# A three-layer graph network on one core: own rows on ScalarE's queue, rows home each six steps, the next team and W2 two steps later

## The chip, the core and the metric

The kernel runs on one NeuronCore of one Trainium2 chip. A core has five engines, each with its own instruction stream in fixed order: TensorE (PE, with the loading of its weights shown apart as PEld), VectorE (DVE), ScalarE (ACT), GpSimd (POOL) and SyncE (SP, which only issues DMAs here). They wait for each other through semaphores. Sixteen DMA engines move data between HBM and the on-chip memory (SBUF). Matrix products land in PSUM, which has eight banks.

The metric is the time of one execution in device microseconds, as the median of several runs.

## What is computed

A graph of 6250 nodes with 256 features and 100000 edges goes through three graph convolutions, and the result is added to the input and normalized:

```python
loops = jnp.arange(n)
src = concatenate([src, loops]); dst = concatenate([dst, loops])
deg = segment_sum(ones_like(dst), dst, n)
dinv = where(deg > 0, rsqrt(deg), 0)
norm_edge = dinv[src] * dinv[dst]
h = x
for W, b in ((W1, b1), (W2, b2), (W3, b3)):      # 256 -> 512 -> 512 -> 256
    h = relu(segment_sum((h @ W)[src] * norm_edge[:, None], dst, n) + b)
return layernorm(x + h)
```

Edges are sorted by `dst`. Each layer is a multiplication of a sparse matrix (edges and self loops) with the rows of all nodes, and one with a weight matrix; the kernel may take them in either order.

## The kernel before

**Tiling.** Nodes lie in 50 blocks of 125. The edges into one block are taken as 16 chunks of 128 edges. For a chunk POOL gathers 128 rows of the layer's table from HBM (L1306, an indirect DMA; in layer 2 a row has 512 numbers, 2 KB), and PE multiplies them with a one-hot matrix that sums them into the block's rows (L1334). To keep precision, ACT casts the gathered rows to a shorter float (L1366, the high half) and DVE subtracts that from the row (L1371, the low half); PE takes both, so a chunk is a pair of products.

**Dense blocks.** For some blocks the sparse matrix is counted out instead: a dense matrix of small integers, kept in HBM as bytes (`kept`). Then the block is a product with all 50 blocks of the table, which are streamed in order. In layer 2 the first 12 blocks are done so, as three *teams* of four (L916): for each source block k, four members get a pair of products (L1005), each into its team's bank. When a team is done, DVE scales its banks into SBUF (L940) and the next team may use them (`take`, L995). The other 38 blocks, 12 to 49, are gathered.

**A block in layer 2.** When a gathered block's sixteen chunks are summed, its *own rows* (the self loops) are added. They are loaded from the table into the one buffer `own_row` (L1321, when chunk j = 10 of the block's 16 is multiplied), scaled by ACT (L1345, with j = 15) and added by DVE (L1472). The next block's own rows can be loaded only then. After that come four transposes (L1426), an ACT copy (L1490), W2 in pairs of blocks (`hidden`, L1499; matmuls L1513), a relu on ACT (L1521), W3 (L1533), a scaling on DVE (L1548), and again a high and a low half (L1558, L1563). The result goes to the table of layer 3 (`tables[2]`) and, for use as dense operand in layer 3, to the SBUF tile `parts`.

**Returns.** While teams run, the upper part of `parts`, behind block 17, holds their buffers. Blocks past 17 that end in that time go to the table alone and come *home* (L1076) after the teams: 25 blocks in runs of up to four. Since the teams' slices and pieces lie in `parts` too, some instructions below carry that name while they move bytes of counts or halves of gathered rows.

**In advance.** Also after the teams, three dense blocks of layer 3 are begun early (`in_advance`, L1027): slices of their counts are loaded (L1036), cast on ACT (L1042, L1045) and multiplied (L1069) with the blocks of `parts` that are already there.

**Order.** All instructions are written by one loop. A *step* is one gathered chunk. Everything else is a generator that says after how many steps it wants to go on; `yield n` puts its next instructions n steps further along in the order of every engine. The constants are `SOON` = 2, `TO_PE` = 5, `LATE` = 6, `RETURN` = 6. In layer 2 a chunk's product stands 10 steps behind its gather; once the last team has six source blocks left, `returning` (L990) is set and the distance shrinks to 6. No cost model and no clock takes part: the order is fixed when the program is built, and at run time each engine waits for what it needs.

**DMA issue.** Most transfers of 125 rows go through `by_rows` (L81), which makes two of them, of 112 and 13 rows; the profile shows them under L85 and L87. Those of SP stand in SP's order, those of ACT in ACT's.

Of the kernel before, what the change touches and what calls it, by code (L numbers as in the profile page):

```python
# [26 lines left out]
Q = 125  # L27
# [4 lines left out]
SOON = 2  # L32
LATE = 6
TO_PE = 5

HOTS = 4
PIECE = 5
# [371 lines left out]
def sorted_path(ctx: ExitStack, tc: tile.TileContext, x, edges, starts, found, wts, biases, room, late, out):  # L409
# [65 lines left out]
    def take(name, most):  # L475
        while held.get(name, 0) >= most:
            yield 1
        held[name] = held.get(name, 0) + 1
# [437 lines left out]
    def teams(groups):  # L916

        nonlocal teams_done, returning
        units = [(g, k) for g in range(len(groups)) for k in range(NB)]

        def fetch_counts(g, c):
            for n, b in enumerate(groups[g]):
                by_rows(nc.sync, team_used[(g * CUTS + c) // 2 % 2][n].rearrange("p k v -> p (k v)"), kept[b][:, c * PIECE * Q:(c + 2) * PIECE * Q])

        def next_counts(g, c):
            if c + 2 < CUTS:
                fetch_counts(g, c + 2)
            elif g + 1 < len(groups):
                fetch_counts(g + 1, c + 2 - CUTS)

        def load(p):
            if 2 * p < len(units):
                k = units[2 * p][1]
                by_rows(nc.sync, streamed[p % RING], tables[1][k * Q:(k + 2) * Q, :].rearrange("(b p) c -> p b c", p=Q))

        def load_scales(g):
            nc.sync.dma_start(out=scales, in_=dinvs[g * TEAM:(g + 1) * TEAM, :].rearrange("b p -> (b p)").unsqueeze(0).to_broadcast([P, TEAM * Q]))

        def scaled(g, n):
            nc.vector.tensor_tensor(team_zt[:, n], team_banks[n][:, :TEAM * Q], scales, op=ALU.mult)  # L940
            free(f"team{n}")
            if n == TEAM - 1:
                if g + 1 < len(groups):
                    load_scales(g + 1)
                yield SOON
                team_ended[0](hidden(groups[g][:2], team_zt[:, :, :2 * Q], "tz"))
                for _ in range(4 * KF if g + 1 < len(groups) else 2 * KF):
                    yield 1
                team_ended[0](hidden(groups[g][2:], team_zt[:, :, 2 * Q:], "tz"))

        def piece(g, c, n):
            nc.scalar.copy(team_pieces[(g * CUTS + c) % 2][:, :, n * Q:(n + 1) * Q], team_used[(g * CUTS + c) // 2 % 2][n][:, c % 2 * PIECE:(c % 2 + 1) * PIECE, :])
            if c % 2 and n == TEAM - 1:
                next_counts(g, c - 1 + 2)

        def half(u, h):
            if u < len(units):
                to, row = both_parts[u % 3], streamed[u // 2 % RING][:, u % 2, :]
                if h == 0:
                    nc.scalar.copy(to[:, :HID], row)  # L960
                else:
                    nc.vector.tensor_sub(to[:, HID:], row, to[:, :HID].bitcast(F32))  # L962

        while products < FEW * NB - HOME // PIECE * PIECE:
            yield 1
        fetch_counts(0, 0)
        for p in range(RING):
            load(p)
        fetch_counts(0, 2)
        yield 6  # L970
        load_scales(0)
        while finished < FEW:
            yield 1
        for bank in team_banks:
            while not any(b is bank for b in common):
                yield 1
            del common[next(n for n, b in enumerate(common) if b is bank)]
        half(0, 0)
        for n in range(TEAM):
            piece(0, 0, n)  # L980
            if n % 2:
                yield 1
        half(0, 1)
        half(1, 0)
        yield 1
        half(1, 1)
        pairs_done = 0
        for u, (g, k) in enumerate(units):
            if u == len(units) - RETURN:
                returning = now  # L990
            if u % 2:
                load((u + 1) // 2 + RING - 1)
            for n in range(TEAM):
                if k == 0:
                    yield from take(f"team{n}", 1)  # L995
                if k == NB - 1 and n == 0:
                    while held.get("tz", 0):
                        yield 1
                    held["tz"] = TEAM // 2
                if 1 <= n < 3:  # L1000
                    half(u + 2, n - 1)
                if k % PIECE == 2 and u + PIECE < len(units):
                    piece(*divmod(g * CUTS + k // PIECE + 1, CUTS), n)
                for h in range(2):
                    nc.tensor.matmul(team_banks[n][:, :TEAM * Q], lhsT=both_parts[u % 3][:, h * HID + n * P:h * HID + (n + 1) * P],  # L1005
                                     rhs=team_pieces[(g * CUTS + k // PIECE) % 2][:, k % PIECE, :],
                                     start=(k == h == 0), stop=(k == NB - 1 and h == 1))
                if k == NB - 1:
                    team_ended[0](scaled(g, n))
                pairs_done += 1  # L1010
                if in_layer == 0 and pairs_done % 3 or in_layer == 1 and (pairs_done % PACE if now >= EAGER else pairs_done % 3 == 0):
                    yield 1
        teams_done = True
        assert not on_loan, (now, len(on_loan))
# [12 lines left out]
    def in_advance():  # L1027

        units = [(m, k) for k in ADVANCE for m in range(BEGUN)]
        banks = [mm_bank, mat_bank, tr_bank]  # L1030
        sliced = [(m, k) for m, k in units if m > 0]

        def load(u):
            if u < len(sliced):
                m, k = sliced[u]
                by_rows(nc.sync, early_slices[u % NS].rearrange("p k v -> p (k v)"), kept[many[m]][:, k * Q:(k + PIECE) * Q])  # L1036

        def convert(u):
            if u < len(units):
                m, k = units[u]  # L1040
                if m == 0:
                    nc.scalar.copy(early_pieces[u % 2], made[:, k:k + PIECE, :])  # L1042
                else:
                    n = sliced.index((m, k))
                    nc.scalar.copy(early_pieces[u % 2], early_slices[n % NS])  # L1045
                    load(n + NS)

        while returning is None:
            yield 1
        by_rows(nc.sync, made.rearrange("p k v -> p (k v)"), kept[many[0]])  # L1050
        for u in range(4):
            load(u)
        while not teams_done:
            yield 1
        for u in range(4, 9):
            load(u)
        while any(held.get(f"team{n}", 0) for n in range(TEAM)):
            yield 1
        for u in range(9, NS):
            load(u)  # L1060
        convert(0)
        yield 1
        sent = 0
        for u, (m, k0) in enumerate(units):
            while any(final.get(k, now + 1) > now for k in range(k0, k0 + PIECE)):
                yield 1
            convert(u + 1)
            for k in range(PIECE):
                nc.tensor.matmul(banks[m][:Q], lhsT=early_pieces[u % 2][:, k, :], rhs=parts[:, k0 + k],  # L1069
                                 start=(advanced[m] == 0), stop=False)  # L1070
                advanced[m] += 1
                sent += 1
                if sent % (2 if u < AT_HOME * BEGUN else AT_ONCE):
                    yield 1

    def home():  # L1076

        while not teams_done or held.get("leaving", 0):
            yield 1
        runs = []  # L1080
        for b in sorted(waiting):
            if runs and runs[-1][-1] == b - 1 and len(runs[-1]) < 4:
                runs[-1].append(b)
            else:
                runs.append([b])
        for run in runs:
            b, e = run[0], run[-1] + 1
            by_rows(nc.sync, parts[:, b:e].bitcast(F32), tables[2][b * Q:e * Q, :].rearrange("(b p) c -> p b c", p=Q))
            final.update((k, now + LANDING) for k in range(b, e))
            yield 4  # L1090

    there = []
    place_of = {}
# [63 lines left out]
    def layer(i, width, gathered, dense, after, rows, first=0, spacing=1.0, extras=(), carried=None):  # L1157
# [151 lines left out]
        def product(c):  # L1309
# [8 lines left out]
                    nc.tensor.matmul(acc[:Q], lhsT=ident_r[:Q, :Q], rhs=parts[:, b], start=True, stop=False)  # L1318
            if i == 1 and j == (3 if b == NB - 1 else KF - LATE):
                assert own_read == b - 1 or b == gathered[0]  # L1320
                by_rows(nc.sync, own_row, tables[1][b * Q:(b + 1) * Q, :])  # L1321
            several = [(j, split_rows.pop(c))]
            if j == KF - 1:
                several.append((KF, of_ten[b // GRP]))
# [174 lines left out]
    def hidden(two, zt, name, win=win_bank, ht2=ht2):  # L1499
# [1 line left out]
        wide = len(two) * Q  # L1501
        each = 4 // len(two)
        shares = win is win_bank
        yield TO_PE
        if shares:
            yield from take("ht2", 1)
        for f2 in range(0, KH, each):
# [348 lines left out]
```

## Time and profile before

| | us |
|---|---|
| median of 3 runs | 2067.19 |
| lowest and highest of them | 2065.59, 2067.45 |
| the profiled execution, its time | 2064.83 |
| its span, first to last instruction | 2063.2 |
| PE busy in it | 1926.2 |
| layer 2, first to last load of own rows | 727 to 1610 |

Times in the profile are in microseconds from the first instruction of the profiled execution. A row of a timeline has the start, the time taken, the engine, the line, the operation, what it writes and reads, and in brackets how long the engine stood idle before it and what ended that. An issue of a DMA is not work of its engine: it is marked with a q (SPq, ACTq), and the transfer ends later. A row of waits has who waited for whom, the total, the number of times and the longest. In a group's row stand the count and the busy time, or the least, the median and the greatest duration.

### The profile page before, as it was taken

The numbers are of one execution on the slowest core, as the hardware profiler recorded it, in microseconds if no ns is written. First come the engines' busy times: TensorE is split into PE (matmuls) and PEld (weight loads), VectorE is DVE, ScalarE is ACT, GpSimd is POOL, SyncE is SP. The second block draws the span as 40 slices with busy tenths as digits, with TensorE's granted clock in tenths as the row PEclk, the third lists the DMA queues.
The fourth block names the chain that finished last, engine by engine and source line by source line (L and its number), as shares of the span: only waits on it lengthen the run. The fifth ranks groups of instructions, "written<-read, shape, count | busy, mean of one in ns | idle before, by whom it ended". The sixth has DMA issues, their size and how long they took to land. (4 is left out here: it accounts for less than half of the span.)

```text
span 2063.2 us, 29141 instructions
## 1 busy us (share of the span) xinstructions
PE 1926.2 (93%) x8679; PEld 1521.4 (74%) x8679; DVE 1379.0 (67%) x2443; ACT 1279.3 (62%) x2255; POOL 1381.4 (67%) x1425
## 2 busy tenths in 40 slices
PE   4399999999999789999999989999889999999997
PEld 3277777777777557778888868888768778788886
DVE  6887888887882376677687676767746445444444
ACT  2566777787875466666676666666656555555553
POOL 2467777766777377777676676766757277777775
PEclk9999999999999899999999999999989999999998
DMA  7898999999999998999999998998997599999997
GB/s 171 246 300 220 264 266 259 272 264 254 276 274 248 250 280 255 267 262 265 263 263 265 263 261 249 267 254 253 266 278 221 151 288 292 289 294 299 290 284 203
DMA packets 266078, 535.53 MB, mean 260 GB/s; under 512 B 44363, under 2 KB 80328, under 8 KB 265910
## 3 DMA queue, kind: packets, MB, share of 16 engines
q0 software_dynamic: 155280, 355.58, 63.3%
q1 hardware_dynamic: 97194, 168.45, 30.3%
q10 hardware_dynamic: 13436, 9.55, 1.8%
q8 instruction: 70, 1.15, 0.2%
q14 instruction: 98, 0.80, 0.1%
HBM read 459.56 MB, written 73.87 MB: 259 GB/s over the span
## 5 line engine op out<-in xcount | busy, mean ns | idle before, releaser
L1306 POOL DMA_INDIRECT room<-tab,ssrc x442 | 456.4, 1033 | 199.8 <-issue 86.2
L1334 PE MATMUL sacc<-halves,shot 128*125 128x512 f32 x1524 | 519.9, 402 | 9.7 <-DMA halves<-tab,ssrc 4.7
L1255 ACT CAST piece<-room 125x625 fp32r<-125x625 uint8 x492 | 350.8, 721 | 187.4 <-PE win_ps L1407 53.0
L1306 POOL DMA_INDIRECT halves<-both,ssrc x384 | 360.5, 939 | 141.9 <-issue 42.4
L1306 POOL DMA_INDIRECT halves<-tab,ssrc x320 | 303.2, 947 | 98.8 <-issue 29.2
L1334 PEld LDWEIGHTS sacc<-halves,shot 128*125 128x125 f32 x1524 | 287.1, 189 | 84.3 <-DVE halves L1371 7.5
L811 DVE TENSOR_TENSOR back<-near_cols,slots 128x625 bf16<-128x625 f32 (+2 forms) x435 | 325.0, 803 | 31.5 <-PE sacc L878 12.4
L1371 DVE TENSOR_TENSOR halves<-room,halves 128x512 fp32r<-128x512 f32 x334 | 226.8, 692 | 121.2 <-ACT halves L1366 118.8
L1246 DVE TENSOR_TENSOR shot<-near_cols,sdlo 128x500 fp32r<-128x500 f32 x366 | 244.9, 670 | 93.2 <-PE sacc L1334 87.6
L1306 POOL DMA_INDIRECT back<-tab,ssrc x230 | 230.9, 1004 | 112.9 <-DVE halves L1371 35.1
L1366 ACT CAST halves<-room 128x512 fp32r<-128x512 f32 x334 | 202.0, 620 | 137.8 <-DMA room<-tab,ssrc 127.8
L1513 PE MATMUL win_ps<-back,w_sb 128*128 128x250 f32 x768 | 183.3, 382 | 9.1 <-ACT back L1490 8.6
L1513 PEld LDWEIGHTS win_ps<-back,w_sb 128*128 128x128 f32 x768 | 148.5, 194 | 33.5 <-ACT back L1490 11.0
L1407 PE MATMUL smm<-parts,piece 125*125 125x512 f32 x565 | 165.9, 409 | 2.1 <-DVE parts L1563 1.2
L1407 PE MATMUL win_ps<-parts,piece 125*125 125x512 f32 x550 | 158.2, 406 | 0.0
L1407 PE MATMUL str<-parts,piece 125*125 125x512 f32 x515 | 149.5, 408 | 0.9 <-ACT piece L1255 0.9
L878 PEld LDWEIGHTS <-back 128*125 128x125 bf16 x725 | 95.9, 138 | 73.3 <-issue 23.0
L1407 PE MATMUL sacc<-parts,piece 125*125 125x512 f32 x450 | 147.7, 432 | 0.9 <-ACT piece L1255 0.9
L840 ACT CAST room<-sacc 125x500 uint8<-125x500 f32 (+1 forms) x155 | 107.7, 713 | 55.3 <-PE sacc L878 40.8
L1371 DVE TENSOR_TENSOR halves<-back,halves 128x512 fp32r<-128x512 f32 x136 | 93.3, 693 | 61.1 <-ACT halves L1366 60.4
L1407 PE MATMUL mat_ps<-parts,piece 125*125 125x512 f32 x415 | 121.3, 408 | 0.4 <-ACT piece L1255 0.4
L962 DVE TENSOR_TENSOR parts<-parts 125x512 fp32r<-125x512 f32 x150 | 103.0, 687 | 25.5 <-ACT parts L960 24.8
(353 smaller groups left out, 3477.5 us busy)
## 6 DMA issues: line engine op xcount, KB each, us to landing
parts<-tab SPq DMA_DIRECT2D x75, 448.0 KB
kept<-room SPq DMA_DIRECT2D x29, 683.6 KB
room<-kept SPq DMA_DIRECT2D x27, 683.6 KB
both<-parts SPq DMA_DIRECT2D x10, 1120.0 KB
tab<-st SPq DMA_DIRECT2D x50, 224.0 KB
own_row<-tab SPq DMA_DIRECT2D x38, 224.0 KB
parts<-kept SPq DMA_DIRECT2D x60, 136.7 KB
room<-tab,ssrc POOLq DMA_INDIRECT x442, 6.2
```

The source lines that it names most:

```text
L811: nc.vector.tensor_tensor(out, near_cols[:, :shape[2]].unsqueeze(1).to_broadcast(shape), numbers.unsqueeze(2).to_broadcast(shape), op=ALU. ...
L840: nc.scalar.copy(place[:, :, u * G:(u + len(ms)) * G].rearrange("p k (t r) -> p t k r", r=G), counted_in[:Q, :len(ms) * 256].rearrange("p ...
L878: nc.tensor.matmul(bank[:Q, len(pair) * 256:][:, :G * NB], lhsT=hot_lo, rhs=hot_key, start=True, stop=True)
L962: nc.vector.tensor_sub(to[:, HID:], row, to[:, :HID].bitcast(F32))
L1246: nc.vector.tensor_tensor(hot[:, :n], near_cols[:, :Q].unsqueeze(1).to_broadcast([P, n, Q]), dlo.rearrange("p b j -> p (b j)")[:, at:at + ...
L1255: nc.scalar.copy(piece[:, :n], made_or_read[:, at:at + n, :])
L1306: nc.gpsimd.indirect_dma_start(out=row, out_offset=None, in_=table, in_offset=bass.IndirectOffsetOnAxis(ap=at, axis=0))
L1334: nc.tensor.matmul(acc[:Q, :size], lhsT=hot, rhs=row[:, c0:c0 + size], start=(i != 0 and k == c0 == 0), stop=(k == KF and c0 + size == row ...
L1366: nc.scalar.copy(halves[:, :width], landed[highs])
L1371: nc.vector.tensor_sub(halves[:, width:], landed.pop(lows), halves[:, :width].bitcast(F32))
L1407: nc.tensor.matmul(acc_d[:Q], lhsT=got[p][:, n, :], rhs=parts[:, k], start=begins and not (i == 2 and m < BEGUN), stop=ends)
L1513: nc.tensor.matmul(h_ps[:, f, :], lhsT=w2_sb[:, k, (f2 + f) * P:(f2 + f + 1) * P], rhs=zt[:, k, :], start=(k == 0), stop=(k == KH - 1))
```

## The change

Five edits in layer 2's order; no arithmetic changes.

```diff
             for n in range(TEAM):
                 if k == 0:
                     yield from take(f"team{n}", 1)
+                    if u and n == 0:
+                        yield SOON
...
         def load(u):
             if u < len(sliced):
                 m, k = sliced[u]
-                by_rows(nc.sync, early_slices[u % NS].rearrange("p k v -> p (k v)"), kept[many[m]][:, k * Q:(k + PIECE) * Q])
+                nc.sync.dma_start(out=early_slices[u % NS].rearrange("p k v -> p (k v)"), in_=kept[many[m]][:, k * Q:(k + PIECE) * Q])
...
             by_rows(nc.sync, parts[:, b:e].bitcast(F32), tables[2][b * Q:e * Q, :].rearrange("(b p) c -> p b c", p=Q))
             final.update((k, now + LANDING) for k in range(b, e))
-            yield 4
+            yield LATE
...
             if i == 1 and j == (3 if b == NB - 1 else KF - LATE):
                 assert own_read == b - 1 or b == gathered[0]
-                by_rows(nc.sync, own_row, tables[1][b * Q:(b + 1) * Q, :])
+                if returning is None:
+                    by_rows(nc.sync, own_row, tables[1][b * Q:(b + 1) * Q, :])
+                else:
+                    nc.scalar.dma_start(out=own_row, in_=tables[1][b * Q:(b + 1) * Q, :])
...
         each = 4 // len(two)
         shares = win is win_bank
-        yield TO_PE
+        yield TO_PE + SOON if shares and not teams_done else TO_PE
```

The second and the third team begin two steps later. The slices of counts come in one transfer of 125 rows each. A return follows the one before after six steps, not four. The own rows of the last seven blocks are asked for by ACT, in one transfer of 125 rows. And while teams run, W2 stands two steps further behind the transposes.

In the rows below, lines of the changed kernel are 2 to 5 higher than those of the kernel before: L1007 is L1005, L1044 and L1047 are L1042 and L1045, L1326 is the new load of own rows, L1339 is L1334, L1350 is L1345, L1371 is L1366, L1518 is L1513, L1563 is L1558.

SP's order where blocks come home, before. `parts<-tab_170` is a return of four blocks, `own_row<-tab_169` the load of own rows, `tab_170<-parts` the store of a pair of finished blocks:

```order
L87 DMA parts<-tab_170 112x4x512
L87 DMA parts<-tab_170 13x4x512
L87 DMA parts<-tab_170 112x4x512
L87 DMA parts<-tab_170 13x4x512
L87 DMA own_row<-tab_169 112x512
L87 DMA own_row<-tab_169 13x512
L87 DMA parts<-tab_170 112x4x512
L87 DMA parts<-tab_170 13x4x512
L85 DMA tab_170<-parts 112x2x512
L85 DMA tab_170<-parts 13x2x512
```

The own rows stand between the second and the third of these returns. The same place of SP's order in the changed kernel:

```order
L87 DMA parts<-tab_170 112x4x512
L87 DMA parts<-tab_170 13x4x512
L87 DMA parts<-tab_170 112x4x512
L87 DMA parts<-tab_170 13x4x512
L85 DMA tab_170<-parts 112x2x512
L85 DMA tab_170<-parts 13x2x512
L87 DMA parts<-tab_170 112x4x512
L87 DMA parts<-tab_170 13x4x512
```

The own rows are no longer between the returns. They stand in ACT's order now, here for the block whose own rows stood in the rows before. `halves` are casts of gathered rows:

```order
L1326 DMA own_row<-tab_169 125x512
L1047 CAST parts<-d 125x625
L1371 CAST halves_6034<-back 128x512
L1371 CAST halves_6035<-room 128x512
L1563 CAST parts<-st 125x2x256
L1371 CAST halves_6028<-room 128x512
L1044 CAST parts<-room 125x625
L1371 CAST halves_6029<-room 128x512
L1371 CAST halves_6030<-room 128x512
L1350 ACTIVATE own_row<-own_row,sdinv 125x512
L1047 CAST parts<-parts 125x625
```

Between the ask and the scaling stand five casts of gathered rows and three other instructions, and behind the scaling the cast of a slice for the early products. In the kernel before, no DMA stands in ACT's order here.

PE's order where the third team begins, before. `str` is the bank of the second team's last member, `sacc_893` that of the third team's first; `win_ps<-back,w_sb` is W2:

```order
L1005 MATMUL str<-parts 128x500 x2
L1334 MATMUL sacc_891<-halves_6028,shot_6023 125x512 x2
L1005 MATMUL sacc_893<-parts 128x500 x2
L1334 MATMUL sacc_891<-halves_6029,shot_6023 125x512 x2
L1513 MATMUL win_ps<-back,w_sb 128x250 x4
L1005 MATMUL mat_ps<-parts 128x500 x2
```

One pair of gathered products stands between the two teams, and W2 behind. In the changed kernel:

```order
L1007 MATMUL str<-parts 128x500 x2
L1339 MATMUL sacc_891<-halves_6030,shot_853 125x512 x2
L1518 MATMUL win_ps<-back,w_sb 128x250 x4
L1339 MATMUL sacc_891<-halves_6031,shot_853 125x512 x2
L1518 MATMUL win_ps<-back,w_sb 128x250 x4
L1339 MATMUL sacc_891<-halves_6032,shot_853 125x512 x2
L1007 MATMUL sacc_893<-parts 128x500 x2
```

Between the two teams stand three pairs of gathered products where one stood, and eight products of W2 that came behind the third team's first before.

## The prediction

> **What bounds the kernel now.** I read the page's busy line first, then busy time by stretch through the second layer, then what PE waited for there, then the timelines around the longest wait.
>
> ```profile
> PE 1926.2 (93%) x8679; PEld 1521.4 (74%) x8679; DVE 1379.0 (67%) x2443; ACT 1279.3 (62%) x2255; POOL 1381.4 (67%) x1425
> 700.00:930.00 230.00, 207.78 (x854) 161.12 (x852) 155.67 (x247) 146.65 (x265) 160.05 (x153) 0.96 0.90 259
> 930.00:1200.00 270.00, 267.41 (x1210) 222.98 (x1210) 198.10 (x314) 181.24 (x333) 189.81 (x187) 1.00 0.93 263
> 1210.00:1440.00 230.00, 230.00 (x1042) 193.31 (x1041) 166.09 (x264) 151.04 (x280) 159.59 (x156) 0.99 0.91 256
> 1500.00:1529.00 29.00, 28.99 (x131) 23.84 (x129) 16.49 (x26) 16.19 (x28) 18.30 (x19) 1.00 1.04 277
> 1529.00:1538.00 9.00, 0.05 (x1) 0.05 (x1) 0.67 (x1) 1.43 (x3) 0.00 (x0) 0.74 1.00 290
> 1538.00:1545.00 7.00, 7.00 (x22) 5.64 (x23) 5.04 (x9) 5.48 (x12) 4.37 (x5) 0.60 1.06 243
> 1545.00:1600.00 55.00, 55.00 (x251) 46.24 (x250) 32.93 (x53) 34.20 (x66) 39.45 (x39) 1.00 0.75 224
> ```
>
> The columns behind the stretch are busy time of PE, weight loads, DVE, ACT and POOL, then PE's granted clock, the DMA engines' busy share and GB/s. PE is busy nearly all the time from 930 us on, while DVE, ACT and POOL have a quarter or more to spare. So an idle microsecond of PE is a microsecond of the kernel, as long as what feeds PE can follow. The exceptions are the first stretch, where PE has other waits (22 us idle of 230), and the hole at 1529: nine microseconds in which PE does nothing while the DMA engines are full (share 1.00), then seven at a clock of 0.60. After it the DMA engines have room (0.75).
>
> ```profile
> PE str L1069 <- ACT parts L1045: 9.0, 1, 9.0
> PE win_ps L1513 <- ACT back L1490: 8.6, 6, 2.4
> PE sacc L1005 <- DVE back L940: 6.4, 2, 5.3
> PE sacc L1426 <- DVE szs L1472: 3.8, 3, 1.5
> PE smm L1069 <- ACT parts L1042: 3.7, 1, 3.7
> ...
> PE win_ps L1513 <- ACT back L1490: 5.6, 4, 2.4
> ```
>
> These are PE's waits in the second layer: total, times, longest (the last row: up to 930 us alone). Three of them are what the change speaks of: the hole (9.0), W2 waiting for the transposed rows (8.6 in six waits), and the next team waiting for DVE to empty its bank (6.4 in two).
>
> The hole's cause stands on SP's, ACT's and PE's timelines.
>
> ```profile
> parts<-tab SPq DMA_DIRECT2D x6, 896.0 KB
> parts<-tab SPq DMA_DIRECT2D x6, 104.0 KB
> ...
> 1503.71 8.79 SPq L87 DMA_DIRECT2D parts<-tab  x4
> 1514.50 1.57 SPq L87 DMA_DIRECT2D own_row<-tab  x2
> 1517.78 5.81 SPq L87 DMA_DIRECT2D parts<-tab  x2
> ...
> 1518.68 0.62 ACT L1366 CAST halves<-back 128x512 fp32r<-128x512 f32 x1 [1.14 <-DMA back<-tab,ssrc]
> ...
> 1524.41 0.62 ACT L1366 CAST halves<-room 128x512 fp32r<-128x512 f32 x1 [0.85 <-DMA room<-tab,ssrc]
> 1536.57 0.72 ACT L1345 ACTIVATE own_row<-own_row,sdinv 125x512 f32<-125x512 f32 x1 [11.54 <-DMA own_row<-tab]
> 1537.20 0.70 ACT L1045 CAST parts<-parts 125x625 fp32r<-125x625 uint8 x1
> ...
> 1528.35 0.64 PE L1334 MATMUL sacc<-halves,shot 128*125 128x512 f32 x2
> 1537.95 0.79 PE L1069 MATMUL str<-parts 125*125 125x512 f32 x1 [8.96 <-ACT parts L1045]
> ```
>
> The first two rows give the size of a return, about 1 MB in two transfers. SP asks for the own rows at 1514.50, behind two returns of 1 MB that were asked for from 1503.71 on. They have landed when ACT starts on them, 22 us later. ACT stops at its scaling, L1345, for 11.54 us, and everything ACT would have done next stops too: the casts of gathered rows, and the cast at L1045 for which PE waits. ACT's last cast ended at 1525.03 and PE ran dry at 1528.99, so PE carries 4.0 us of a stop of ACT: that cover is used below.
>
> That it is the queue and not the DMA engines alone shows in the gathers of the same stretch, which POOL issues on a queue of its own, about as large (128 rows of 2 KB):
>
> ```profile
> DMA to landing us min/median/max: 8.0/8.6/9.7
> ...
> DMA to landing us min/median/max: 3.4/4.1/7.5
> ```
>
> The first line is for the gathers asked for between 1500 and 1527, the second for those between 1540 and 1610. In the crowded stretch they land after 8.6 us, and the own rows after 22.
>
> The Trainium skill, "DMA: Bandwidth & Descriptors", section "Issuing engines are not separate DMA queues", speaks against this part of the change: all issuers share the same 16 engines, and asking from another saves only the time of issuing. By that rule the own rows would still land after some 22 us and T1 below would be nothing. The trace does not agree so far: 8.6 against 22 us in the same stretch, on two queues.
>
> **The change, part by part.** The sum is made against the profiled execution, 2064.83 us (span 2063.2); the median of the three runs lies 2.36 us above it.
>
> *T1, own rows on ACT's queue, and returns each six steps.* Seven of the 38 loads move, the ones after the last team nears its end. Gone is the hole, 8.96 us, and the slow stretch behind it: 7.00 us at 0.60 is 2.8 us lost. Together 11.8. What is late next? ACT now asks five steps ahead of its own use. In the rows above that is from 1518.68 (the fifth cast before) to 1525.03, 6.4 us. If the rows land as the gathers do, in 8.6 us, ACT waits 2.2 us, under the cover of 4.0; from 1540 on they land in 4.1 and nobody waits. No row shows how long one transfer of 125 rows takes; its bounds are the 3.4 us of the fastest gather and the 22 us of the old ask. I take the gathers' median, as the nearest in size, place and having its own queue. ACT also issues: seven times the row below, 2.5 us in all, on an engine that is idle for 21 of the 55 us after 1545.
>
> ```profile
> L85 ACTq DMA_DIRECT2D out<-st x100: 322/354/1030, 1661.1 to 2058.2; - x100
> ```
>
> The new ask stands in ACT's order, so it must also wait for DVE to have read the rows before (L1472). That read stands five to six steps earlier and so is done; behind the ask wait the casts, were it not.
>
> But 9 us of hole were not empty for the DMA engines: at 290 GB/s they moved 2.6 MB, mostly returns, which must now share the engines with gathers. With six steps between returns instead of four, some of that goes into the stretch at 0.75, where at 224 GB/s of the 290 seen there are 66 GB/s free, 3.6 MB in 55 us. It fits, though not all at the right time: I take two thirds of 11.8, **8 us**, with 0 and 11.8 as its ends.
>
> *T2, the next team two steps later.* It comes twice; the longer wait is the second row below. In two steps PE has two more pairs of products to do first:
>
> ```profile
> 1620.66 4.99 PE L1334 MATMUL sacc<-halves,shot 128*125 128x512 f32 x20
> 1208.05 1.18 PE L1005 MATMUL sacc<-parts 125*128 125x500 f32 x2 [5.35 <-DVE back L940]
> 1209.87 3.12 PE L1513 MATMUL win_ps<-back,w_sb 128*128 128x250 f32 x8
> ```
>
> Four at 0.25 us are 1.0 us of cover at each place: **2 us** of the 6.4. At 1208 the eight of W2 move ahead of the team too, but they need an ACT copy that is itself late there, so I count nothing for them. The ends are 0, if those products are late too, and 6.4.
>
> *T3, W2 two steps later.* Two steps hold two pairs of products and two pairs of the team's, 8 at about 0.25 us, 2.0 us of cover. The longest of the six waits is 2.4 us, so nearly all of 8.6 could go. Four of the six, 5.6 us, lie before 930, where PE has other waits close behind, so I take half, **4 us**; the ends are 0 and 8.6.
>
> *Nothing from the rest.* The 14 slices of counts are asked for in one transfer instead of two. SP saves 14 issues and half of the places in flight; their first use is far behind, some 47 us for the first four (rows below: asked from 1450, the first cast at 1497), and this hides a slower landing. The last team ends four steps later and the early products with it; PE has the same work, and the program still places all of it inside the second layer, whose last gathers' products fill PE to the end. The wait of 3.7 us for L1042 comes from a late gather in ACT's order ahead of it, during the first return, which stays: nothing.
>
> ```profile
> 1450.09 9.52 SPq L87 DMA_DIRECT2D d<-kept  x8
> 1486.68 0.83 SPq L87 DMA_DIRECT2D parts<-tab  x2
> 1494.90 0.62 ACT L1366 CAST halves<-room 128x512 fp32r<-128x512 f32 x1 [2.88 <-DMA room<-tab,ssrc]
> 1495.43 0.71 ACT L1042 CAST parts<-room 125x625 fp32r<-125x625 uint8 x1
> 1496.83 0.71 ACT L1045 CAST parts<-d 125x625 fp32r<-125x625 uint8 x1
> ```
>
> Sum: 8 + 2 + 4 = 14 us; 2064.8 − 14 = 2050.8, and on the median 2067.2 − 14 = **2053**.
>
> **The rivals.**
>
> *The wait only moves (no change).* If the DMA engines bound the whole end, the hole's 2.6 MB push the gathers back by as much. For it: shares of 1.00 to 1.06 from 1500 to 1545. Against it: 0.75 right after, and PE without a wait from 1500 to 1529 beside a share of 1.04. T1 gives nothing, and T2 and T3 vanish into the same queue: about 2065.
>
> *The change does not do what it says.* The own rows land as late from ACT's queue as from SP's: T1 is nothing, T2 and T3 stay: 2067.2 − 6 = 2061. The gathers' 8.6 us speak against it.
>
> *Slower: the ask blocks ACT.* One transfer of 125 rows may land later than two of 112 and 13, on top of the crowd, and ACT, in order, stops at L1345 once per block, seven times. PE loses what exceeds 6.4 + 4.0 = 10.4 us of landing. The change's other gains are 11.8 + 2 + 4 = 17.8, so it turns slower when PE loses over 2.5 us each time, with landings over **12.9 us**. At 15.4, midway from 8.6 to 22, PE loses 5 us seven times: 2067 + 35 − 18 = 2084. For it: 22 us have been seen for this very load. Against it: that was behind 2 MB on one queue, and four of the seven fall where gathers land in 4.1.
>
> The Trainium skill, same page, section "Why a DMA increments its semaphore by 16 and not by 1", gives a reason for this rival: a transfer is split over the largest number up to 16 that divides its slowest dimension, which is 5 engines for 125 rows and 16 for 112. No run here shows it. By that rule each of five engines carries 25 rows in place of about 8, an estimate of three times the data time, which in the crowded stretch would put the landing beyond the point that decides.
>
> **How the numbers follow.** The forecast, PE idle gone in part, 2040 to 2061: 0.70. The wait moves, 2063 to 2069: 0.13. The own rows as late as before, 2061: 0.07. ACT blocked, 2070 to 2090: 0.10. All three terms at their upper ends give 26.8 us, 2040. The range reaches from there, a microsecond lower, to 2067, and leaves out the slower case, the upper part of no change and a rest below. A measurement can tell about 0.2% from no change, 4.1 us. Faster: 0.70 + 0.07 = 0.77; within: 0.13; slower: 0.10.
>
> **What would show it.** Right: no PE wait over 3 us between 1500 and 1560 and no clock under 0.9 there; ACT's wait for own rows under 2.5 us each; `win_ps L1513 <- ACT back L1490` under 4 us in all; returns spread over some 50 us. Wrong: seven waits of ACT at its scaling, each over 4 us (the slower case); gathers that land in over 10 us until 1600 with PE waiting for casts (the wait moved); a PE hole before L1069 as long as now. A return landing after its first use would be a new wait, of PE for `parts<-tab`, that none of these cases holds.

## The result, and the profile after

| | us |
|---|---|
| kernel before, median of 12 runs | 2063.98 |
| changed kernel, median of 12 runs | 2072.83 |
| ratio of the runs, 95% interval | 1.0055 [1.0040, 1.0069] |
| the profiled execution after, its time and span | 2081.1, 2079.4 |

The change made the kernel slower, by about 9 us between the medians and by 0.55%, some 11 us, in the ratio of the runs. The forecast was 2053 us, and the time lies above its range. The profiled execution is 8 us slower than the median of its kernel, so it is read for where the waits are, and the sizes are taken from the ratios.

The busy line of the page and the stretches of layer 2's end, in the columns of the prediction:

```profile
PE 1936.2 (93%) x8679; PEld 1518.0 (73%) x8679; DVE 1379.7 (66%) x2443; ACT 1281.5 (62%) x2255; POOL 1384.4 (67%) x1425
1480.00:1501.00 21.00, 20.30 (x91) 16.05 (x89) 12.98 (x21) 10.32 (x19) 14.07 (x14) 1.00 0.94 252
1501.00:1512.00 11.00, 0.67 (x2) 0.35 (x3) 6.53 (x11) 4.22 (x8) 4.73 (x5) 0.67 0.70 227
1512.00:1519.00 7.00, 7.00 (x26) 5.73 (x27) 4.47 (x7) 4.14 (x8) 4.58 (x5) 0.79 0.60 147
1519.00:1553.00 34.00, 33.20 (x151) 27.08 (x150) 16.08 (x25) 17.79 (x32) 18.86 (x19) 1.00 1.04 270
1553.00:1580.00 27.00, 21.13 (x77) 15.69 (x76) 14.97 (x23) 14.00 (x26) 14.27 (x16) 0.87 0.79 226
```

The hole at 1529 is gone, PE works from 1519 to 1553 beside full DMA engines. But a hole of about the same length stands at 1501 and six more microseconds are missing after 1553. The new hole ends with the first of the early products, where the kernel before waited 3.7 us. And the second row has something that the old hole did not have: while PE waited, the DMA engines were at 0.70, where they had been at 1.00. So PE's wait did not come from 16 engines that were all busy.

PE's waits of 1480 to 1645 in the changed kernel, who waited for whom, the total, the times and the longest:

```profile
PE smm L1071 <- ACT parts L1044: 13.7, 2, 10.3
PE mat_ps L1071 <- ACT parts L1047: 2.3, 2, 1.6
```

ACT's wait for own rows there, and then ACT's timeline around the first three asks and scalings:

```profile
ACT own_row L1350 <- DMA own_row<-tab: 14.0, 3, 5.6
```

```profile
1497.23 0.26 ACTq L1326 DMA_DIRECT2D own_row<-tab  x1
1499.51 0.62 ACT L1371 CAST halves<-room 128x512 fp32r<-128x512 f32 x1 [1.68 <-DMA room<-tab,ssrc]
...
1504.17 0.62 ACT L1371 CAST halves<-room 128x512 fp32r<-128x512 f32 x1 [0.23 <-DMA room<-tab,ssrc]
1510.37 0.72 ACT L1350 ACTIVATE own_row<-own_row,sdinv 125x512 f32<-125x512 f32 x1 [5.58 <-DMA own_row<-tab]
1510.99 0.70 ACT L1044 CAST parts<-room 125x625 fp32r<-125x625 uint8 x1
...
1527.51 0.26 ACTq L1326 DMA_DIRECT2D own_row<-tab  x1
...
1540.89 0.72 ACT L1350 ACTIVATE own_row<-own_row,sdinv 125x512 f32<-125x512 f32 x1 [3.88 <-DMA own_row<-tab]
...
1557.69 0.26 ACTq L1326 DMA_DIRECT2D own_row<-tab  x1
1570.39 0.72 ACT L1350 ACTIVATE own_row<-own_row,sdinv 125x512 f32<-125x512 f32 x1 [4.54 <-DMA own_row<-tab]
```

And the row of PE's timeline that ends the hole:

```profile
1511.74 0.79 PE L1071 MATMUL smm<-parts 125*125 125x512 f32 x1 [10.33 <-ACT parts L1044]
```

Three of the seven own rows now stop ACT, for 14.0 us in all. From ask to scaling they took 13.1, 13.4 and 12.7 us, and each scaling began as its rows landed. The cast that PE waits for stands right behind the first of these scalings. ACT's stop is 5.6 us of the 10.3: PE had run dry at 1501.41, 3.4 us before ACT's last cast ended at 1504.79. The second stop cost PE almost nothing (33.20 of 34 us busy from 1519 on). PE's waits for casts of slices add up to 16.0 us (13.7 + 2.3) where they were 12.7 (9.0 + 3.7). The gathers, of 128 rows, landed in 8.2 and 9.1 us. The first row is for those asked for from 1485 to 1512, the second from 1512 to 1553:

```profile
DMA to landing us min/median/max: 6.4/8.2/8.8
DMA to landing us min/median/max: 3.9/9.1/10.6
```

### The profile page after: what moved, and what is told of

It is laid out like the page before. It is cut to its first block, busy times and chain, and to the rows that moved or that the text cites. A ratio compares the mean times of both kernels' runs of the same rounds, so it can differ in the third digit from the quotient of the medians.

```text
span 2079.4 us, 29088 instructions
## 1 busy us (share of the span) xinstructions
PE 1936.2 (93%) x8679; PEld 1518.0 (73%) x8679; DVE 1379.7 (66%) x2443; ACT 1281.5 (62%) x2255; POOL 1384.4 (67%) x1425
## 4 chain that ended last, share of the span: by engine, by line
PE 57%; DMA 17%; issue 10%; POOL 6%; ACT 4%; DVE 3%; SPq 0%; ACTq 0%; POOLq 0%; DVEq 0%
PE sacc L1339 10%; DMA room<-tab,ssrc 9%; PE smm L1412 6%; PE str L1412 6%; PE win_ps L1412 5%; PE sacc L1412 5%; DMA back<-tab,ssrc 4%; PE mat_ps L1412 4%; POOL room L1308 4%; PE win_ps L1518 3%; PE sacc L1457 2%; PE win_ps L1538 2%; POOL back L1308 1%; PE sacc L878 1%; DMA halves<-tab,ssrc 1%
## 5 line engine op out<-in xcount | busy, mean ns | idle before, releaser
L1339 PE MATMUL sacc<-halves,shot 128*125 128x512 f32 x1524 | 518.9, 401 | 11.9 <-DMA halves<-tab,ssrc 6.3
L1339 PEld LDWEIGHTS sacc<-halves,shot 128*125 128x125 f32 x1524 | 285.4, 187 | 89.2 <-DVE halves L1376 7.8
L1371 ACT CAST halves<-room 128x512 fp32r<-128x512 f32 x334 | 202.1, 620 | 148.3 <-DMA room<-tab,ssrc 133.7
L1518 PE MATMUL win_ps<-back,w_sb 128*128 128x250 f32 x768 | 186.0, 386 | 7.9 <-ACT back L1526 4.5
L1518 PEld LDWEIGHTS win_ps<-back,w_sb 128*128 128x128 f32 x768 | 149.7, 196 | 33.5 <-ACT back L1526 6.5
```

The lines of the kernel that those rows point to most:

```text
L1339: nc.tensor.matmul(acc[:Q, :size], lhsT=hot, rhs=row[:, c0:c0 + size], start=(i != 0 and k == c0 == 0), stop=(k == KF and c0 + size == row ...
L1371: nc.scalar.copy(halves[:, :width], landed[highs])
L1518: nc.tensor.matmul(h_ps[:, f, :], lhsT=w2_sb[:, k, (f2 + f) * P:(f2 + f + 1) * P], rhs=zt[:, k, :], start=(k == 0), stop=(k == KH - 1))
```

## The experiments

Four theories stood at the start. **Theory 1**: one transfer of 125 rows is slow by its shape and stops ACT. **Theory 2**: the slices in one transfer are slow in the same way, or make gathers late. **Theory 3**: the two shifts cost. **Theory 4**: the returns each six steps cost. The first kernels start from the change and undo one part, the later ones start from the kernel before and do one part. Runs of one group were on one chip; in the last three groups they were chips on which the kernel before takes 2259 to 2287 us, so only ratios within a group are compared there. In the traces from those chips PE also has waits for which the profile shows no cause (21.8 us before one line in own_128_shifts), so an effect need not have the same size on both kinds of chip.

### From the changed kernel: rows and slices

`own_two` (own rows on ACT's queue in two transfers):

```diff
-                    nc.scalar.dma_start(out=own_row, in_=tables[1][b * Q:(b + 1) * Q, :])
+                    by_rows(nc.scalar, own_row, tables[1][b * Q:(b + 1) * Q, :])
```

> After the change, but ScalarE asks for an own row in two transfers (112 rows and 13) in place of one of 125. Theory 1 (one transfer of 125 rows is itself slow: asked at 1497 to 1558 us it was there 13 us later, while gathers of 128 rows took 8 to 9): own rows land in 7 to 9 us, ACT's three waits at its scaling (14.0 us) shrink under 5 us, PE's hole of 10.3 us before L1071 shrinks, ratio to before 0.997 to 1.001. Theory 2 (the slices in one transfer make the gathers late from 1484 on, and the hole is theirs): the hole stays over 7 us, ratio 1.003 to 1.006. Theory 3 (the two-step shifts cost the time): own rows may land sooner, but the ratio stays at 1.004 or above and PE waits for ACT's relu before W2 stay at 8 us.

`slices_two` (the slices of counts in two transfers, as before):

```diff
-                nc.sync.dma_start(out=early_slices[u % NS].rearrange("p k v -> p (k v)"), in_=kept[many[m]][:, k * Q:(k + PIECE) * Q])
+                by_rows(nc.sync, early_slices[u % NS].rearrange("p k v -> p (k v)"), kept[many[m]][:, k * Q:(k + PIECE) * Q])
```

> After the change, but each slice of counts is asked for in two transfers (112 rows and 13), as before the change. Theory 2 (slices in one transfer make the gathers late): ACT's waits for gathers between 1485 and 1502 us (2.8, 2.4 and several of 1 us) fall to those of the kernel before, and the hole of 10.3 us shrinks under 4 us; ratio to before 0.997 to 1.002. Theory 1 (only the own row's single transfer): ACT still waits 4 to 6 us at its scaling, the hole keeps over 7 us, ratio 1.003 to 1.006.

`both_two` has both edits.

> After the change, with both own rows and slices in two transfers of 112 and 13 rows; what is left of the change is ScalarE's queue, the returns each six steps and the two shifts. Theories 1 and 2 together: no PE wait over 4 us between 1490 and 1560 us, ratio to before 0.992 to 0.998 (the 8 to 12 us of the hole). Theory 3 (the shifts cost) or a theory 4 (returns each six steps cost): ratio 1.002 or above although the waits for own rows are gone.

`own_128` (one transfer, three rows more; `own_row` is the first 125 rows of `own_full`):

```diff
-                    nc.scalar.dma_start(out=own_row, in_=tables[1][b * Q:(b + 1) * Q, :])
+                    wide = Q if b == NB - 1 else P
+                    nc.scalar.dma_start(out=own_full[:wide], in_=tables[1][b * Q:b * Q + wide, :])
```

> After the change, but ScalarE asks for 128 rows in one transfer (three more than are used; the last block 125), still one transfer. If it is the number of rows that makes it slow (125 rows dividing badly over the DMA engines; 128 evenly), own rows land in 7 to 9 us, as in two transfers, and ACT's waits at its scaling fall under 5 us in all. If it is one transfer as such, or ACT's queue, that is slow, they land after 12 to 14 us as in the changed kernel, and the ratio stays 1.004 to 1.007.

| kernel | median, us | ratio to before, 95% | ACT's waits for own rows in the profile, us |
|---|---|---|---|
| changed kernel | 2072.83 | 1.0055 [1.0040, 1.0069] | 14.0 |
| slices_two | 2071.72 | 1.0037 [1.0021, 1.0054] | 8.5 |
| own_two | 2066.91 | 1.0011 [0.9992, 1.0031] | 2.1 |
| both_two | 2066.60 | 1.0008 [0.9990, 1.0025] | 1.2 |
| own_128 | 2060.81 | 0.9981 [0.9962, 1.0001] | 1.7 |

Three rows more make the changed kernel 12 us faster (2072.83 − 2060.81, medians of two groups; the two ratios lie 0.74% apart). That is theory 1, and it is the number of rows, not one transfer as such. Slices in two change nothing beyond the intervals, alone or with the own rows: theory 2 is not the cause, though an effect of 0.1 or 0.2% would not show. Both_two was expected at 0.992 to 0.998 with no wait of PE over 4 us; it came out at 1.0008 with one of 7.3 us: with both mended the loss is gone, but the gain is still missing.

The traces put the difference at the end of layer 2. From the scaling of the ninth-last own row to that of the last, one execution each took 192.0 us in the kernel before, 199.7 in the changed kernel, 197.6 in slices_two, 191.5 in own_two, 190.0 in both_two and 189.9 in own_128.

Why three rows matter shows in the count of packets on ACT's DMA queue (q10), over the time in which one own row was moved. The view of the DMA queues has packets, MB and the share of 16 engines. In the changed kernel from 1532 to 1541 us:

```profile
q10 hardware_dynamic: 130, 0.26, 9.0%
```

In own_128 from 1528 to 1533:

```profile
q10 hardware_dynamic: 144, 0.26, 16.7%
```

In own_two from 1525.5 to 1530.5:

```profile
q10 hardware_dynamic: 154, 0.26, 19.7%
```

A row of 2 KB is one packet, so there are 5 packets beyond 125 rows, 16 beyond 128, and 29 = 16 + 13 beyond 112 + 13. The packets' times in the traces, for the same three loads:

```
                 rows  packets beyond  first to last packet, us  rows under way at once, at most
changed kernel    125        5                7.82                         5
own_128           128       16                4.12                        13
own_two           125       29                4.17                        12
```

So 125 rows in one transfer went over few engines, by the extra packets five with 25 rows each, and took about twice as long (8.04 and 7.74 us in the other two loads that stopped ACT). This load stood in the crowd of returns and gathers. Outside it up to 7 of the rows were under way at once and a load took 3.0 to 4.0 us, where own_128 had up to 18 and 1.3 to 2.4 us, and ACT was not stopped. The Trainium skill, "DMA: Bandwidth & Descriptors", section "Why a DMA increments its semaphore by 16 and not by 1", says that each engine in a transfer ends its part with a write to the semaphore, and that their number is the largest up to 16 that divides the slowest dimension: 5 for 125, 16 for 128 and 112, 13 for 13. The counts 5, 16 and 29 are those numbers: the trace agrees. The share of 0.70 fits too, but which engines were idle the trace does not tell.

PE's wait for L1044 from 1480 to 1645, in own_two:

```profile
PE smm L1071 <- ACT parts L1044: 8.7, 2, 6.6
```

and in own_128:

```profile
PE smm L1071 <- ACT parts L1044: 3.4, 2, 2.0
```

In own_two 6.6 us of hole are left at 1505 although ACT waited only 1.1 us for its own row. Most of its casts just before had waited 0.6 to 1.3 us each for a gather, behind the first return of 1 MB. That part of the hole is not the own rows'. This wait, of PE for the first early product, was 3.7, 2.9 and 4.9 us in the three kernels without the two shifts (before, own_128_no_shifts, own_128_alone). With the shifts it was 6.6 here, 7.5, 7.3 and 6.0 in slices_two, both_two and own_128_each_four, but 4.4 in shifts_alone and 2.0 in own_128. So the shifts are a suspect; what sets it was not tried.

### One part at a time

`shifts_alone` is the kernel before with the two shifts:

```diff
                     yield from take(f"team{n}", 1)
+                    if u and n == 0:
+                        yield SOON
...
-        yield TO_PE
+        yield TO_PE + SOON if shares and not teams_done else TO_PE
```

> The kernel before with the two shifts alone (next team and W2 two steps later); own rows, slices and returns as before. Prediction's terms T2 and T3: 6 us less, ratio 0.996 to 0.998. Rival (the wait only changes its name: W2 then waits for ScalarE's relu in place of its copy, some 8 us of the changed kernel's waits): ratio 0.999 to 1.002. Theory 3 (the shifts cost): 1.003 or above. The hole of 9 us at ScalarE's scaling of own rows stays in all three.

`own_128_no_shifts` is own_128 without these lines.

> As own_128, without the two shifts: own rows by 128 rows on ScalarE's queue, returns each six steps, slices in one transfer. If the shifts are worth their 6 us: ratio to before 1.000 to 1.003 (own_128 had 0.998). If they only change the name of a wait: 0.997 to 0.999, as own_128. If they cost: 0.994 to 0.996.

`own_128_each_four` is own_128 with `yield 4` between returns.

> As own_128, with returns each four steps as before the change. If the wider spacing carries the gain (the crowd of returns and gathers from 1500 us on): a PE hole of over 5 us comes back between 1500 and 1560 us, gathers land after 10 us or more there, ratio 1.000 to 1.004. If the own rows' queue alone removed the hole: PE's waits there stay under 4 us each, ratio 0.997 to 0.999.

`own_128_alone` is the kernel before with one edit:

```diff
-                by_rows(nc.sync, own_row, tables[1][b * Q:(b + 1) * Q, :])
+                if returning is None:
+                    by_rows(nc.sync, own_row, tables[1][b * Q:(b + 1) * Q, :])
+                else:
+                    wide = Q if b == NB - 1 else P
+                    nc.scalar.dma_start(out=own_full[:wide], in_=tables[1][b * Q:b * Q + wide, :])
```

> The kernel before with one edit: from the last team's end on ScalarE asks for own rows, 128 rows in one transfer. The prediction's T1 without the wider returns: the 11.5 us wait at ScalarE's scaling falls under 3 us, PE's hole of 9.0 us goes; ratio 0.995 to 0.998 (4 to 10 us of 2064). Rival (the DMA engines bound the end, the wait moves into gathers): own rows land in 6 to 8 us but PE waits as long for casts, ratio 0.999 to 1.001.

| kernel | median, us (before: 2062.98) | ratio, 95% |
|---|---|---|
| shifts_alone | 2067.02 | 1.0026 [1.0012, 1.0041] |
| own_128_no_shifts | 2058.72 | 0.9975 [0.9958, 0.9993] |
| own_128_each_four | 2060.28 | 1.0000 [0.9982, 1.0018] |
| own_128_alone | 2055.46 | 0.9974 [0.9960, 0.9987] |

`own_128_alone` beats both kernels. Its last nine scalings span 186.5 us, 5.5 less than before. PE's waits in it from 1480 to 1645:

```profile
PE smm L1069 <- ACT parts L1042: 4.9, 1, 4.9
PE sacc L1338 <- DMA halves<-tab,ssrc: 1.6, 1, 1.6
PE str L1069 <- ACT parts L1045: 1.4, 2, 1.1
```

and its gathers asked for between 1500 and 1527:

```profile
DMA to landing us min/median/max: 8.4/9.0/11.0
```

ACT waits 0.4 us for own rows in all. PE's wait of 9.0 has become 1.4, the other one stays (3.7 before, 4.9 now). The gathers land 0.4 us later than in the kernel before (9.0 against 8.6): the hole's bytes did not come back as late gathers. So the prediction's T1, with rows that land as gathers do, is real: 5.4 us by the ratio (0.26% of 2063, the interval from 2.7 to 8.3), where 8 were taken.

The shifts gain nothing: beside own rows of 128 there is no difference that could be told (0.9981 with, 0.9975 without, in different groups), and alone they cost 0.26% (its last nine scalings span 197.6 us, 192.0 before). The spacing of returns can't be told from nothing by these four. Own_128_each_four has a hole of over 5 us again, as its expectation said for the case that the spacing matters, but at 1496 and with no stop of ACT by own rows before it.

### Rows and queue

`own_125_alone` is own_128_alone with the change's own line (125 rows in one transfer on ACT's queue), `own_two_alone` has `by_rows(nc.scalar, ...)` there, `own_128_on_sync` has `nc.sync` in place of `nc.scalar`, and `own_128_home_six` adds `yield LATE` between returns.

> The kernel before with the own rows as the change asks for them and nothing else: from the last team's end on ScalarE asks for 125 rows in one transfer. Own_128_alone, three rows more, had 0.9974. Theory 1 (125 rows go over five DMA engines, land after 12 to 14 us and stop ScalarE): ScalarE waits 3 to 6 us at its scaling in three of seven blocks, ratio 1.002 to 1.006. Rival (ScalarE's queue is worth what it was with 128 rows, and the loss of the changed kernel needs the other edits): ratio 0.996 to 0.999.

> As own_128_alone, but the one transfer of 128 rows stays on SyncE's queue. If it is the queue that made the own rows late before (asked for behind 2 MB of returns): ScalarE still waits over 5 us at its scaling once or twice, ratio 0.999 to 1.002. If one transfer of 128 rows in place of two of 112 and 13 did it: waits under 2 us, ratio 0.996 to 0.998 as own_128_alone.

> As own_128_alone, but two transfers of 112 and 13 rows on ScalarE's queue. If the queue is what counts: own rows land in 7 to 8 us, ScalarE's waits stay under 2 us, ratio 0.996 to 0.999. If the single even transfer is needed (own_two had 1.0011 where own_128 had 0.9981): 0.999 to 1.002.

> Own_128_alone with returns each six steps. If the wider spacing helps (own_128 0.998 against own_128_each_four 1.000): ratio to before 0.994 to 0.996. If it is nothing: 0.9965 to 0.9985. If a return now lands after its first use (PE waited 4.4 us for it in own_128_no_shifts): such a wait of 3 us or more shows again, ratio 0.998 to 1.000.

Since the first two intervals hold no change, the first two came again on another chip, with 125 rows on SP's queue (`own_125_on_sync`, `nc.sync` in the change's line) and own_128_alone with the two shifts (`own_128_shifts`).

> Own_125_alone once more, beside the same load in three other forms on one chip. Theory 1 (125 rows on five DMA engines stop ScalarE): 1.002 to 1.006, ScalarE's waits at its scaling over 8 us in all. Rival (on ScalarE's queue 125 rows are as good as 128): 0.996 to 0.999, waits under 3 us.

> The kernel before with own rows of 125 in one transfer from the last team's end on, but on SyncE's queue. If rows and queue add: it lands after 22 us or later, as in the kernel before, and more often; ratio 1.002 to 1.008. If the queue alone decides (rows don't matter there, since all transfers wait behind the returns): 0.999 to 1.002, as before. If the number of transfers is what counts on SyncE: below 0.999, as own_128_on_sync.

> Own_128_on_sync on the chip of the three others. If the queue is what made the own rows late: they land 15 us or more after the ask and ScalarE waits over 5 us once; ratio 0.999 to 1.002. If one even transfer is enough on either queue: 0.996 to 0.999.

> Own_128_alone (0.9974) with the two shifts. If the shifts are worth the 6 us of the prediction's T2 and T3: 0.994 to 0.996. If they only rename waits: 0.996 to 0.999. If they cost, as shifts_alone's 1.0026 says: 0.999 to 1.001, with early products that end some 7 us later and the last two blocks of gathers 3 us longer.

| kernel | ratio, 95% (group with before at 2286.62) | ratio, 95% (group with before at 2258.65) |
|---|---|---|
| 125 rows in one, ACT's queue | 1.0016 [0.9996, 1.0036] | 1.0027 [1.0005, 1.0050] |
| 125 rows in one, SP's queue | | 1.0025 [1.0003, 1.0047] |
| 128 rows in one, SP's queue | 0.9987 [0.9964, 1.0011] | 1.0014 [0.9982, 1.0045] |
| 112 and 13 rows, ACT's queue | 0.9969 [0.9944, 0.9994] | |
| 128 rows, ACT's queue, returns each six | 0.9984 [0.9964, 1.0003] | |
| 128 rows, ACT's queue, shifts | | 1.0031 [1.0007, 1.0055] |

On ACT's queue the same rows make the kernel faster in two transfers and not in one of 125: 0.9969 against 1.0016 beside each other (0.9974 for 128, on another chip). On SP's queue 128 rows stay within their intervals of no change. Why, shows in asks and scalings. ACT's timeline in own_125_alone:

```profile
1669.30 0.26 ACTq L1324 DMA_DIRECT2D own_row<-tab  x1
1685.81 0.72 ACT L1348 ACTIVATE own_row<-own_row,sdinv 125x512 f32<-125x512 f32 x1 [8.11 <-DMA own_row<-tab]
```

SP's in own_128_on_sync, asks for two blocks:

```profile
1640.92 0.34 SPq L1325 DMA_DIRECT2D own_row<-tab  x1
1668.97 0.34 SPq L1325 DMA_DIRECT2D own_row<-tab  x1
```

and ACT's in the same run, their scalings:

```profile
1661.64 0.72 ACT L1349 ACTIVATE own_row<-own_row,sdinv 125x512 f32<-125x512 f32 x1 [1.35 <-DMA own_row<-tab]
1687.14 0.73 ACT L1349 ACTIVATE own_row<-own_row,sdinv 125x512 f32<-125x512 f32 x1 [2.91 <-DMA own_row<-tab]
```

125 rows landed 16.5 us after the ask (1669.30 to 1685.81), and 128 on SP's queue 20.7 and 18.2 us. So the change mended the queue and broke the shape: in the crowd either alone is enough to make the rows late. It is not so for each load. In own_125_alone this one of the seven stopped ACT, in its repetition again one, for 4.7 us, less than the 3 to 6 us in three blocks and the 8 us in all that were expected. The changed kernel and slices_two, with returns each six steps, had three stops each. On SP's queue 128 rows stopped ACT for 4.3 us in own_128_on_sync and 5.9 in its repetition. The Trainium skill, "DMA: Bandwidth & Descriptors", section "Issuing engines are not separate DMA queues", allows only the time of issuing as a gain from another queue. The traces speak against it here: even 128 rows took 18 to 21 us on SP's queue, behind returns asked for from 1631.85 and 1658.07 us on, and on ACT's, in own_128_home_six on the same chip, the rows for the same two blocks were scaled about 9 us after their asks (1669.25 to 1678.34, 1694.47 to 1703.52). In own_two_alone, also on that chip and with returns each four steps as in own_128_on_sync, it was 9.5 and 9.1 us.

The returns each six steps show no gain (0.9984 with 128 rows, beside 0.9969 with each four and 112 + 13 rows, in the same group). Theory 4 is not shown either way; the intervals overlap.

### Which shift

`team_shift_alone` and `w2_shift_alone` are the kernel before with the first or the second half of shifts_alone's diff.

> The kernel before with T2 alone: the next team's first product two steps later. T2 as predicted: 2 us less, 0.998 to 1.000. If this is the half that makes the two shifts cost (1.0026 and, beside own rows of 128, 1.0031): 1.001 to 1.004, with early products ending later.

> The kernel before with T3 alone: W2 two steps later while teams run. T3 as predicted: 4 us less, 0.997 to 0.999, W2's waits for ScalarE's copy under 4 us. If this is the half that costs: 1.001 to 1.004, with W2's waits for the relu in place of those for the copy. If both halves cost: both runs at 1.001 to 1.002.

They gave 1.0000 [0.9974, 1.0026] and 1.0008 [0.9985, 1.0032] (before: 2261.99): neither can be told from no change. That together they gain nothing is shown three times (shifts_alone, own_128 against own_128_no_shifts, own_128_shifts). That they cost rests on shifts_alone alone. Own_128_shifts (1.0031) points the same way, but own rows of 128 without the shifts were not run on its chip, and the pair of own_128 shows no cost. Through which of the two, stays open.

## Why the prediction was wrong

**T1, the step that failed.** "No row shows how long one transfer of 125 rows takes ... I take the gathers' median, as the nearest in size, place and having its own queue": 8.6 us. In the three loads that stopped ACT, measured were 12.7 to 13.4, on both sides of the 12.9 us that the prediction had worked out as the turning point. What was nearest in size was not near in shape: a gather has 128 rows. The rival "the ask blocks ACT" had the mechanism, and the sentence on the skill beside it had the reason (five engines in place of 16; the estimate of three times the data time came out as 1.9, 7.82 us against 4.12). It got 0.10, its price taken midway to 22 us and at seven blocks. In the trace three of the seven were stopped; the other four have no wait, as the prediction said of blocks outside the crowd. But the crowd did not end at 1540, from where the prediction had nobody waiting: the third load that stopped ACT was asked for at 1557.69. And the cover of 4.0 us was there at the second stop, not at the first, where PE was dry before ACT stopped. That the time lies in the rival's 2070 to 2090 is in part luck, as the next term lost too. With rows that land as gathers do T1 is worth 5.4 us. With 125 in one transfer, alone, the ratios are 1.0016 and 1.0027 (own_125_alone, twice; the first interval holds no change). So what stood as a gain of 8 us was a loss, of some 3 to 6 us if those ratios hold on the first chips.

**T2 and T3, 6 us.** The waits that they named did shrink, and others took their place. W2's wait for the relu in the kernel before, then PE in the changed kernel, both from 680 to 1490 us:

```profile
PE win_ps L1513 <- ACT back L1521: 0.5, 1, 0.5
```

```profile
PE sacc L1457 <- ACT back L1451: 7.6, 1, 7.6
...
PE win_ps L1518 <- ACT back L1526: 3.8, 3, 1.7
PE win_ps L1538 <- ACT back L1526: 3.6, 5, 1.8
PE win_ps L1518 <- ACT back L1495: 3.2, 3, 2.0
...
PE sacc L1007 <- DVE back L940: 0.2, 1, 0.2
```

W2's wait for ACT's copy fell from 8.6 to 3.2, under the 4 that were to show T3 right. But PE now waits for the relu behind W2 (L1526): 7.4 us (3.8 + 3.6) where it was 0.5. The next team's wait for DVE fell from 6.4 to 0.2, and yet the kernel with both shifts is no faster. The sum did not fall. Up to 1480 us all of PE's waits are 37.4 us before and 37.2 in the changed kernel. On the first chips they are 30.3 to 40.9 in the three kernels without the shifts and 31.9 to 39.9 in the seven with them, one execution each. So rows of one execution are too uncertain for terms of 2 and 4 us. A wait that goes is not a term of the sum until it is said what is late next; for T3 the prediction did not.

**The sum of the parts.** Own rows as asked for +0.16 to +0.27%, the shifts alone +0.26%, slices nothing: 0.42 to 0.53%, of 0.55 measured. The parts were timed in different groups, on both kinds of chip, and their intervals are about as wide as they are, so this is a check and no proof.

**What held.** The returns spread, from 1486.98 to about 1543 us, and the hole at 1529 went. "Nothing from the rest": slices in one transfer change nothing measurable (own_two against both_two, 1.0011 and 1.0008). The wait of 3.7 us for L1042 stayed in own_128_alone (4.9); in the changed kernel, where the prediction also let it stay, it is the one that grew to 10.3. The rival that the wait only moves, into gathers, falls with own_128_alone.

## What to carry to other kernels

Before two transfers are made one, look at what the number of rows divides into: here, beside full DMA engines, 125 rows in one took about 7.8 us to move, by the packets over five engines, and 128 rows, three of them unused, or 112 and 13 took 4.1 to 4.2. For the load that ACT, an in-order engine, waits for here, its own queue and an even shape were both needed. And where an edit takes a wait away, write down what the next instruction of that chain waits for before counting the gain.

## What was not expected of the hardware

The own rows have a queue of their own on ACT, and still hold up SP. In SP's waits of the changed kernel between 1480 and 1645 us one return waits for them:

```profile
SPq L87 <- DMA own_row<-tab: 2.9, 1, 2.9
```

The trace has this return waiting for the semaphore on which ACT's DMA of the own rows reports, although it neither reads nor writes their buffer. The wait ended at 1540.86 us, just before the scaling of these rows.
